# Graph attention in three layers: units of up to five chunks, weights in SBUF, second PSUM banks for R

## The chip, the cores and the metric

The kernel runs on one core of a Trainium2 chip. The time is device microseconds of one execution, from several executions of the same program. Five engines work side by side and meet at semaphores: TensorE (PE; its weight loads are listed as PEld), VectorE (DVE), ScalarE (ACT), GpSimd (POOL) and SyncE (SP). SP and POOL issue the DMAs: SP the plain ones, POOL the gathers of rows by an index list.

## The reference, cut to what matters

Four layers run over a graph of 3327 nodes with 512 features: `x = x + layer(relu(layernorm(x)), adj)`. Layers 0, 2 and 3 are graph attention with 8 heads of 64, layer 1 averages neighbours. The attention of layer 3, to which the others are alike:

```python
hp = jnp.einsum('nd,hdf->hnf', h, W)
f_src = jnp.einsum('hnf,hf->hn', hp, a_src)
f_dst = jnp.einsum('hnf,hf->hn', hp, a_dst)
e = jax.nn.leaky_relu(f_src[:, :, None] + f_dst[:, None, :], ALPHA)
e = jnp.where(adj[None] > 0, e, NEG_FILL)
att = jax.nn.softmax(e, axis=-1)
out = jnp.einsum('hij,hjf->hif', att, hp)
```

The adjacency is sparse and skewed: a node's chance of an edge falls with its number, so the first nodes have many neighbours and the last ones few.

## The kernel before

Since the exponential of a leaky ReLU of a sum is the larger of two products, each factor known per node, the weight of an edge from j to i is, but for factors of i that the softmax divides out, the larger of a value R of the target i and a value T of the source j, times exponentials that are put into the source's row beforehand. So each layer first writes a `table` with one row of 528 numbers per node: 8 heads x (64 features + 1), scaled, and 8 values T. (Layer 0 has 104 further words per row with the adjacency as bits.) R goes to `r_dram` in one form and stays in SBUF as `r3`, three bf16 parts, in another.

Targets are taken in groups of 64 (`GB`), two groups to a block of 128, 52 groups in all. `PLAN` gives for each group how many chunks of 128 source rows it reads: `dense` (128 consecutive nodes, a plain DMA), `mixed` and `pure` (gathers by the index list). There are 368 chunks per layer: 150 dense and mixed ones, called slots, where a source may reach any of the 64 targets, and 218 pure ones, where each row is one edge. `Lists.units` (L585) cuts a group's slots into units of at most `SLOTS` and its edges into units of at most `UNIT`, as even as can be. `ls.order` alternates blocks with many chunks and blocks with few.

`attend` (L1347) runs over the units in that order, for layers 0, 2 and 3. The order of the instructions on TensorE, VectorE and ScalarE is the order in which the code records them; GpSimd and SP run ahead on their own queues until a buffer is not free.

- `load` (L1444) fetches a unit's rows into `rows_e` (edges) or `rows_s` (slots), three units ahead in the text; how far the gathers run ahead in time is a matter of the buffers.
- A slot unit: VectorE takes the larger of R, broadcast to all partitions in PSUM as `r_bc` by `spread` (L1374), and T, into `mx` in PSUM (L1581), and multiplies by the 0/1 mask into `wgt` in SBUF (L1585). TensorE multiplies, head by head, `wgt` by the rows and adds into `facc` (L1616; 16 instructions a chunk).
- An edge unit: `pick` (L1506) selects R of each edge's target with a 0/1 matrix `edges` on TensorE, into `r_of` in PSUM, two units ahead; `summed` (L1517) adds R's three parts into `w_of` on VectorE, just behind the work of the unit before; then the larger of `w_of` and T (L1568), and `vw`, the rows times that weight (L1571). TensorE sums `vw` over the targets with the 0/1 matrix `ones_of` (L1605; 4 instructions a chunk).
- In layer 0 the 0/1 matrices are made from the bits: `bits` (L1461, VectorE), `masks` (L1478 to L1483, ScalarE), and for edges `turned` (L1493, TensorE) and `kept` (L1502, ScalarE and a DMA), three units ahead. Layers 2 and 3 read what layer 0 kept.
- At a group's end `ending` copies the sums (L1419), divides (L1425, L1432) and goes through the layer's finish (L1656 to L1663), one step per unit, called by `later`.
- `tick`, called once per unit too, drives work for the next layer: in layer 0 batch statistics with 26 GpSimd operations `bn_d` (L1715), in layer 2 the projection of finished blocks (`Following`), eight steps a block; the next block starts when the one before has taken `lag` steps. When the loop is over, `hurry` gives it three PSUM banks of the loop's and the remaining blocks follow.

PSUM has eight banks. In layer 2 they are two of `facc`, two of `mx`, one `r_bc`, one `r_of`, two of the projection. `w_of` shares `mx`'s buffer (`mx[:, 0, :UNIT, :H]`).

## Time and profile before

| | us |
|---|---|
| median of 4 runs | 2625.29 (2622.69 to 2633.84) |
| the profiled execution | 2648.22 |
| its span | 2646.4 |
| lists and the projection of layer 0 | 0 to about 337 |
| loop of layer 0 | 337 to 896 |
| batch statistics, layer 1 | 896 to 1512 |
| loop of layer 2 | 1512 to 2079 |
| the last projections of layer 2 | 2079 to 2125 |
| loop of layer 3 and its end | 2123 to 2646 |

The span runs from the first to the last instruction of the program; the execution's time has what lies around it as well. Engine busy times overlap. "Idle" in the profile is an engine's time without work just ahead of an instruction, and the arrow names what ended most of it; an end of a matmul is modelled there, so that a wait for TensorE is often put down to the instruction beside the one that released it. DMA_INDIRECT is one gather of 128 rows; its duration is GpSimd's part, not the transfer.

The DMA issues of the loops, by size:

```profile
rows_s<-table SPq DMA_DIRECT2D x46, 528.0 KB
rows_s<-table SPq DMA_DIRECT2D x62, 264.0 KB
rows_e<-table,idx POOLq DMA_INDIRECT x654
rows_s<-table,idx POOLq DMA_INDIRECT x219
```

### The profile page before, as it was taken

The numbers are of one execution on the slowest core, as the hardware profiler recorded it, in microseconds if no ns is written. First come the engines' busy times: TensorE is split into PE (matmuls) and PEld (weight loads), VectorE is DVE, ScalarE is ACT, GpSimd is POOL, SyncE is SP. The second block draws the span as 40 slices with busy tenths as digits, with TensorE's granted clock in tenths as the row PEclk, the third lists the DMA queues.
The fourth block names the chain that finished last, engine by engine and source line by source line (L and its number), as shares of the span: only waits on it lengthen the run. The fifth ranks groups of instructions, "written<-read, shape, count | busy, mean of one in ns | idle before, by whom it ended". The sixth has DMA issues, their size and how long they took to land. (4 is left out here: it accounts for less than half of the span.)

```text
span 2646.4 us, 42809 instructions
## 1 busy us (share of the span) xinstructions
PE 2006.4 (76%) x14843; PEld 1126.9 (43%) x14843; DVE 1698.6 (64%) x3056; ACT 1095.6 (41%) x4124; POOL 1152.0 (44%) x1205
## 2 busy tenths in 40 slices
PE   5887767778777499778989758888888756767675
PEld 4654344445444243223333245454444344444342
DVE  5567867776667680234454567777767467878776
ACT  3564113445454452122222204567777503344343
POOL 0000045566555202655666345554555045555552
PEclk9788868888888799989999877788888867777676
DMA  7685188767767384756777787776767177777773
GB/s 310 232 303 165 62 296 245 236 205 220 210 202 236 102 276 160 234 180 203 224 226 235 226 243 212 223 211 203 212 210 217 50 256 225 246 229 214 213 244 96
DMA packets 204943, 561.86 MB, mean 212 GB/s; under 512 B 36985, under 2 KB 42745, under 8 KB 201392
## 3 DMA queue, kind: packets, MB, share of 16 engines
q0 software_dynamic: 93120, 327.86, 41.1%
q1 hardware_dynamic: 111600, 231.20, 25.8%
q8 instruction: 120, 1.97, 0.3%
q14 instruction: 103, 0.84, 0.1%
HBM read 496.07 MB, written 62.86 MB: 211 GB/s over the span
## 5 line engine op out<-in xcount | busy, mean ns | idle before, releaser
L1342 POOL DMA_INDIRECT rows_e<-table,idx x654 | 623.8, 954 | 716.0 <-DMA rows_s<-table 330.6
L1605 PE MATMUL facc<-vw,ones_of 128*64 128x260 f32 x2616 | 501.2, 488 | 100.7 <-DVE vw L1571 59.6
L1616 PE MATMUL facc<-rows_s,wgt 128*64 128x65 f32 x7200 | 403.9, 257 | 225.8 <-issue 137.8
L1616 PEld LDWEIGHTS facc<-rows_s,wgt 128*64 128x64 f32 x7200 | 335.6, 165 | 348.2 <-issue 228.5
L1342 POOL DMA_INDIRECT z_rows<-z_dram,idx x291 | 277.1, 952 | 299.4 <-DMA z_dram<-z_out 130.9
L1571 DVE TENSOR_TENSOR vw<-rows_e,w_of 128x1040 f32<-128x1040 f32 (+1 forms) x270 | 395.7, 1466 | 9.3
L1342 POOL DMA_INDIRECT rows_s<-table,idx x219 | 211.8, 967 | 395.7 <-PE facc L1616 235.5
L1585 DVE TENSOR_TENSOR wgt<-mx,mask 128x1024 f32<-128x1024 f32 (+1 forms) x255 | 280.3, 1099 | 86.9 <-ACT mask L1483 26.2
L1581 DVE TENSOR_TENSOR mx<-r_bc,rows_s 128x1024 f32<-128x1024 f32 (+1 forms) x255 | 280.6, 1100 | 74.3 <-DMA rows_s<-table 16.3
L1605 PEld LDWEIGHTS facc<-vw,ones_of 128*64 128x64 f32 x2616 | 215.3, 166 | 255.4 <-issue 159.4
L1432 ACT ACTIVATE fhp<-sums,rd 64x64 f32<-64x64 f32 x816 | 215.6, 334 | 228.8 <-DVE rd L1425 152.3
L1523 DVE TENSOR_REDUCE w_of<-r_of 128x16 f32<-128x48 f32 (+1 forms) x270 | 61.4, 227 | 230.1 <-PE r_of L1515 57.3
L1866 PE MATMUL sage_acc<-z_rows,z_mask 128*64 128x512 f32 x622 | 167.2, 607 | 9.5 <-DMA z_rows<-z_dram,idx 7.1
L1849 ACT CAST z_mask<-mask 128x128 f32<-128x128 uint8 (+1 forms) x201 | 51.2, 287 | 231.0 <-PE sage_acc L1866 135.4
L921 PE MATMUL p_wh<-fWt,hT 128*128 128x512 f32 x208 | 107.5, 665 | 39.0 <-ACT hT L916 32.0
L1419 ACT COPY sums<-facc 128x260 f32<-128x260 f32 x153 | 56.3, 368 | 192.3 <-PE facc L1616 145.6
L739 PE MATMUL wh_ps<-fWt,hT 128*128 128x512 f32 x208 | 116.3, 711 | 0.0
L1515 PE MATMUL r_of<-r_three,edges 64*128 64x24 bf16 x654 | 61.0, 178 | 64.2 <-ACT edges L1502 31.8
L1432 ACT ACTIVATE bn_y<-sums,rd 64x64 f32<-64x64 f32 x408 | 107.7, 334 | 2.6 <-DVE rd L1425 1.0
L978 PE MATMUL p_wh<-fWt,hT 128*128 128x512 f32 x184 | 106.7, 733 | 0.6 <-issue 0.6
L1502 ACT CAST edges<-st_ps 64x384 bf16<-64x384 f32 (+1 forms) x90 | 37.0, 411 | 162.1 <-PE st_ps L1493 75.2
L1817 DVE TENSOR_TENSOR s_o<-n_ps,sage_b 128x512 f32<-128x512 f32 x26 | 18.0, 690 | 132.8 <-PE n_ps L1814 76.1
(252 smaller groups left out, 2949.2 us busy)
## 6 DMA issues: line engine op xcount, KB each, us to landing
adj_i<-in_adj SPq DMA_DIRECT2D x26, 1664.0 KB
rows_s<-table SPq DMA_DIRECT2D x46, 528.0 KB
table<-v_row SPq DMA_DIRECT2D x78, 264.0 KB
rows_s<-table SPq DMA_DIRECT2D x62, 264.0 KB
rows_s<-table SPq DMA_DIRECT2D x23, 632.0 KB
fin_x<-fx SPq DMA_DIRECT2D x52, 256.0 KB
rows_e<-table,idx POOLq DMA_INDIRECT x654
rows_s<-table SPq DMA_DIRECT2D x31, 316.0 KB
```

The source lines that it names most:

```text
L739: nc.tensor.matmul(wh, hT[:, kc, :], self.Wt[:, kc, :], start=(kc == 0), stop=(kc == KC - 1))
L921: nc.tensor.matmul(wh, hT[:, kc, :], self.Wt[:, kc, :], start=(kc == 0), stop=(kc == KC - 1))
L978: nc.tensor.matmul(wh, hT[:, kc, :], self.Wt[:, kc, :], start=(kc == 0), stop=(kc == KC - 1))
L1342: nc.gpsimd.indirect_dma_start(out=dst, out_offset=None, in_=src[:, :], in_offset=bass.IndirectOffsetOnAxis(ap=idx[:, k : k + 1], axis=0))
L1432: nc.scalar.mul(hp[o0 : o0 + GB, h * F : (h + 1) * F], sm[mine, q, 0:F], rd[mine, q, :])
L1523: nc.vector.tensor_reduce(w[:, :n], re[:, :n].rearrange("p k (t h) -> p k h t", h=H), AX.X, ALU.add)
L1571: nc.vector.tensor_tensor(vw[:, :n], gt[:, :n, : H * (F + 1)].rearrange("p k (h x) -> p k h x", x=F + 1), w[:, :n].unsqueeze(3).to_broadca ...
L1581: nc.vector.tensor_tensor(mx[:, :n], rbs[j].unsqueeze(1).to_broadcast(full), T.unsqueeze(3).to_broadcast(full), ALU.max)
L1585: nc.vector.tensor_tensor(wt[:, :n], mx[:, :n], mk.unsqueeze(2).to_broadcast(full), ALU.mult)
L1605: nc.tensor.matmul(accs[g][v * GB : (v + 1) * GB, :sw].rearrange("p (q x) -> p q x", x=F + 1), ones_of[i][:, k, :], by[:, v], start=f, stop=l,
L1616: nc.tensor.matmul(accs[g][v * GB : (v + 1) * GB, q * (F + 1) : (q + 1) * (F + 1)], wt[:, k, h, :], gt[:, k, h * (F + 1) : (h + 1) * (F + 1)],
L1866: nc.tensor.matmul(acc[u * GB : (u + 1) * GB, :], m, z, start=f, stop=l)
```

## The change

`SLOTS` and `UNIT` are now given by layer: slot units of up to 2, 3 and 4 chunks and edge units of up to 4, 5 and 5 in layers 0, 2 and 3, where they were 2 and 3 in all. `mx` is gone: the larger of R and T is written into `wgt` in SBUF and multiplied by the mask in place. `w_of` is an SBUF tile of its own. The two banks of `mx` go to a second `r_bc` and a second `r_of`. Row buffers: edges 3 (were 5 in layer 0 and 6 in the others), slots 4 (4 and 5); `vw` and `wgt` have 2 everywhere (were 3 in layers 2 and 3); `ones_of` 4 (5). `lag` in layer 2 is 4 (5), and `hurry` hands over one bank of `r_of` and two of `r_bc`.

```diff
--- before.py
+++ after.py
@@ -68,8 +68,7 @@
 NSHIFT = 8
 LNB = 5
 ROW = H * (F + 1) + H
-UNIT = 3
-SLOTS = 2
+SLOTS, UNIT = {0: 2, 2: 3, 3: 4}, {0: 4, 2: 5, 3: 5}
 AHEAD = 3
 HOT = 2
 EPARTS = 5
@@ -582,11 +581,11 @@
         src += [(False, k * HALF + g) for k in range(pure)]
         return [(self.at[g] + i, d, k) for i, (d, k) in enumerate(src)]
 
-    def units(self, g):
+    def units(self, g, slots, unit):
 
         dense, mixed, pure = PLAN[g]
         rows, out = self.rows(g), []
-        for edge, part, most in ((False, rows[: dense + mixed], SLOTS), (True, rows[dense + mixed :], UNIT)):
+        for edge, part, most in ((False, rows[: dense + mixed], slots), (True, rows[dense + mixed :], unit)):
             n, at = -(-len(part) // most), 0
             for b in range(n):
                 w = len(part) // n + (b < len(part) % n)
@@ -1350,11 +1349,11 @@
 
 
 
-        width = table.shape[1]
+        width, slots, unit = table.shape[1], SLOTS[layer], UNIT[layer]
         groups = [b * PG + u for b in ls.order for u in range(PG)]
         units = []
         for j, g in enumerate(groups):
-            mine = ls.units(g)
+            mine = ls.units(g, slots, unit)
             spread_at = sum(not e for e, _, _ in mine) - 1
             units += [(j, g, e, rows, s0, i == 0, i == len(mine) - 1, i == spread_at) for i, (e, rows, s0) in enumerate(mine)]
         hq = H // PG
@@ -1363,7 +1362,7 @@
             name=f"facc_ps{layer}", bufs=2, space=PSUM
         ) as aps, tc.manual_schedule(engines={ET.PE, ET.DVE, ET.Activation}):
             loaded, ones_of, st_of, found, w_of, rrs, rbs, accs, ends, over = {}, {}, {}, {}, {}, {}, {}, {}, [], []
-            ahead = 2
+            ahead, wide = 2, 2
 
             def fetch(j):
                 if j < len(groups):
@@ -1375,7 +1374,7 @@
 
 
                 if j < len(groups):
-                    rb = aps.tile([P, H * GB], F32, name="r_bc", tag="r_bc", bufs=1)
+                    rb = aps.tile([P, H * GB], F32, name="r_bc", tag="r_bc", bufs=wide)
                     nc.tensor.matmul(rb, ones[0:2, :].bitcast(F32R), rrs.pop(j).bitcast(F32R), start=True, stop=True)
                     rbs[j] = rb.rearrange("p (h i) -> p h i", i=GB)
 
@@ -1446,9 +1445,9 @@
                 if i < len(units):
                     _, _, e, rows, _, _, _, _ = units[i]
                     if e:
-                        gi = ap.tile([P, UNIT, width], I32, name="rows_e", tag="rows_e", bufs=5 if layer == 0 else 6)
+                        gi = ap.tile([P, unit, width], I32, name="rows_e", tag="rows_e", bufs=3)
                     else:
-                        gi = ap.tile([P, SLOTS, width], I32, name="rows_s", tag="rows_s", bufs=4 if layer == 0 else 5)
+                        gi = ap.tile([P, slots, width], I32, name="rows_s", tag="rows_s", bufs=4)
                     loaded[i] = gi
                     take(gi, table, rows)
 
@@ -1457,7 +1456,7 @@
                 if layer == 0 and i < len(units):
                     _, g, _, rows, _, _, _, _ = units[i]
                     n, nw = len(rows), GB // WB
-                    on = ap.tile([P, UNIT, nw, WB], U16, name="on", tag="on")
+                    on = ap.tile([P, unit, nw, WB], U16, name="on", tag="on")
                     nc.vector.tensor_tensor(
                         on[:, :n],
                         loaded[i][:, :n, ROW:].bitcast(U16)[:, :, g * nw : (g + 1) * nw].unsqueeze(3).to_broadcast([P, n, nw, WB]),
@@ -1473,7 +1472,7 @@
                     n, m0 = len(rows), rows[0][0]
                     mk = mask[:, m0 : m0 + n, :]
                     if e:
-                        so = ones_of[i] = ap.tile([P, UNIT, GB], F32, name="ones_of", tag="ones_of", bufs=5)
+                        so = ones_of[i] = ap.tile([P, unit, GB], F32, name="ones_of", tag="ones_of", bufs=4)
                         if layer == 0:
                             nc.scalar.activation(so[:, :n, :], on, AF.Sign)
                             nc.scalar.copy(mk, so[:, :n, :])
@@ -1488,7 +1487,7 @@
                     _, g, _, rows, _, _, _, _ = units[i]
                     u = g % PG
                     mine = slice(u * GB, (u + 1) * GB)
-                    st = st_of[i] = aps.tile([P, UNIT, P], F32, name="st_ps", tag="st_ps", bufs=1)
+                    st = st_of[i] = aps.tile([P, unit, P], F32, name="st_ps", tag="st_ps", bufs=1)
                     for k in range(len(rows)):
                         nc.tensor.matmul(st[mine, k, :], ones_of[i][:, k, :], cs["ident"], start=True, stop=True)
 
@@ -1498,7 +1497,7 @@
                     _, g, _, rows, s0, _, _, _ = units[i]
                     u, n = g % PG, len(rows)
                     mine = slice(u * GB, (u + 1) * GB)
-                    to = ap.tile([P, UNIT, P], BF16, name="edges", tag="edges", bufs=3)
+                    to = ap.tile([P, unit, P], BF16, name="edges", tag="edges", bufs=3)
                     nc.scalar.copy(to[mine, :n, :], st_of[i][mine, :n, :])
                     nc.sync.dma_start(edges_dram[mine, s0 : s0 + n, :], to[mine, :n, :])
                     st_of[i] = to[mine, :n, :]
@@ -1510,7 +1509,8 @@
                     b, u = divmod(g, PG)
                     mine = slice(u * GB, (u + 1) * GB)
                     st = st_of.pop(i) if layer == 0 else edges[mine, s0 : s0 + len(rows), :]
-                    re = found[i] = aps.tile([P, UNIT, 3 * H], F32, name="r_of", tag="r_of", bufs=1)
+                    bank = aps.tile([P, BANK], F32, name="r_of", tag="r_of", bufs=wide)
+                    re = found[i] = bank[:, : unit * 3 * H].rearrange("p (k x) -> p k x", x=3 * H)
                     for k in range(len(rows)):
                         nc.tensor.matmul(re[:, k, :], st[:, k, :], r3[mine, b, :], start=True, stop=True)
 
@@ -1518,8 +1518,7 @@
 
                 if i < len(units) and units[i][2]:
                     n, re = len(units[i][3]), found.pop(i)
-                    mx = aps.tile([P, SLOTS, H, GB], F32, name="w_of", tag="mx", bufs=1)
-                    w = w_of[i] = mx[:, 0, :UNIT, :H]
+                    w = w_of[i] = ap.tile([P, unit, H], F32, name="w_of", tag="w_of")
                     nc.vector.tensor_reduce(w[:, :n], re[:, :n].rearrange("p k (t h) -> p k h t", h=H), AX.X, ALU.add)
 
             for j in range(2):
@@ -1566,7 +1565,7 @@
                 if e:
                     w = w_of.pop(i)
                     nc.vector.tensor_tensor(w[:, :n], w[:, :n], T, ALU.max)
-                    vw = ap.tile([P, UNIT, H, F + 1], F32, name="vw", tag="vw", bufs=2 if layer == 0 else 3)
+                    vw = ap.tile([P, unit, H, F + 1], F32, name="vw", tag="vw")
                     full = [P, n, H, F + 1]
                     nc.vector.tensor_tensor(
                         vw[:, :n],
@@ -1577,12 +1576,11 @@
                 else:
                     mk = mask[:, m0 : m0 + n, :]
                     full = [P, n, H, GB]
-                    mx = aps.tile([P, SLOTS, H, GB], F32, name="mx", tag="mx", bufs=1)
+                    wt = ap.tile([P, slots, H, GB], F32, name="wgt", tag="wgt")
                     nc.vector.tensor_tensor(
-                        mx[:, :n], rbs[j].unsqueeze(1).to_broadcast(full), T.unsqueeze(3).to_broadcast(full), ALU.max
+                        wt[:, :n], rbs[j].unsqueeze(1).to_broadcast(full), T.unsqueeze(3).to_broadcast(full), ALU.max
                     )
-                    wt = ap.tile([P, SLOTS, H, GB], F32, name="wgt", tag="wgt", bufs=2 if layer == 0 else 3)
-                    nc.vector.tensor_tensor(wt[:, :n], mx[:, :n], mk.unsqueeze(2).to_broadcast(full), ALU.mult)
+                    nc.vector.tensor_tensor(wt[:, :n], wt[:, :n], mk.unsqueeze(2).to_broadcast(full), ALU.mult)
                 summed(i + 1)
                 early(i)
                 if begins:
@@ -1630,9 +1628,7 @@
                     ends.append(ending(g))
             over.append(True)
             if beside is not None:
-                mx = aps.tile([P, SLOTS, BANK], F32, name="mx", tag="mx", bufs=1)
-                rb = aps.tile([P, BANK], F32, name="r_bc", tag="r_bc", bufs=1)
-                beside.hurry((mx[:, 0, :], mx[:, 1, :], rb))
+                beside.hurry([aps.tile([P, BANK], F32, name=k, tag=k, bufs=wide) for k in ("r_of", "r_bc", "r_bc")])
             while ends or (beside is not None and beside.busy()):
                 later()
 
@@ -1875,7 +1871,7 @@
     edges = epool.tile([P, ls.ne, P], BF16, name="edges")
     with ExitStack() as l3:
         at2 = proj
-        proj = following(l3, 3, 2, t["L3_gnn_W"], 2, 5)
+        proj = following(l3, 3, 2, t["L3_gnn_W"], 2, 4)
         attend(2, at2.table, at2.r_dram, at2.r3, elu_into(x2, x3, proj.begin), proj.tick, beside=proj, edges=edges)
     attend(3, proj.table, proj.r_dram, proj.r3, elu_into(x3, out), edges=edges)
```

## The prediction

> **What bounds the kernel now.** I read the page's totals first, then the busy time of each engine by stretch, then the groups of instructions with shapes kept apart, then the waits, then the timeline instruction by instruction.
>
> ```profile
> span 2646.4 us, 42809 instructions
> PE 2006.4 (76%) x14843; PEld 1126.9 (43%) x14843; DVE 1698.6 (64%) x3056; ACT 1095.6 (41%) x4124; POOL 1152.0 (44%) x1205
> ```
> ```profile
> core 0: us, PE busy (x) PEld busy (x) DVE busy (x) ACT busy (x) POOL busy (x), PEclk, DMA share, GB/s
> 336.60:896.00 559.40, 408.54 (x4065) 266.80 (x4067) 393.76 (x664) 248.44 (x832) 307.96 (x316) 0.83 0.72 220
> 1511.70:2078.90 567.20, 452.81 (x4022) 270.54 (x4023) 405.07 (x699) 331.84 (x1339) 276.69 (x288) 0.81 0.70 212
> 2078.90:2125.50 46.60, 24.54 (x71) 12.40 (x67) 14.58 (x44) 17.07 (x84) 5.02 (x6) 0.72 0.21 79
> 2122.90:2627.00 504.10, 346.13 (x3541) 216.19 (x3541) 388.55 (x539) 174.14 (x589) 276.19 (x288) 0.73 0.73 223
> ```
>
> The three attention loops (layers 0, 2, 3) take 559 + 567 + 504 = 1630 us, 62% of the span; the change touches nothing else, except the 46.6 us between the last matmul of layer 2's loop and the first of layer 3's. No engine is full in them. VectorE (DVE) works 70%, 71% and 77% of the three loops, TensorE 73%, 80% and 69%; the rest is waiting of one for the other.
>
> ```profile
> L1523 DVE TENSOR_REDUCE w_of<-r_of 128x16 f32<-128x48 f32 x156 | 33.8, 217 | 165.8 <-remote 45.2 <-PE r_of L1515 45.0 <-PE facc L1616 24.0
> L1523 DVE TENSOR_REDUCE w_of<-r_of 128x24 f32<-128x72 f32 x114 | 27.6, 242 | 64.4 <-PE facc L1616 28.5 <-PE r_of L1515 12.3 <-PE st_ps L1493 9.8
> L1568 DVE TENSOR_TENSOR w_of<-w_of,rows_e 128x16 f32<-128x16 f32 x156 | 28.3, 182 | 3.1 <-DVE rd L1425 0.4 <-DVE w_of L1523 0.3
> L1571 DVE TENSOR_TENSOR vw<-rows_e,w_of 128x1560 f32<-128x1560 f32 x114 | 202.8, 1779 | 3.9
> L1571 DVE TENSOR_TENSOR vw<-rows_e,w_of 128x1040 f32<-128x1040 f32 x156 | 192.9, 1237 | 5.4
> L1585 DVE TENSOR_TENSOR wgt<-mx,mask 128x1024 f32<-128x1024 f32 x195 | 238.8, 1225 | 64.9 <-PE facc L1616 20.6 <-remote 18.8 <-ACT mask L1483 11.5
> L1585 DVE TENSOR_TENSOR wgt<-mx,mask 128x512 f32<-128x512 f32 x60 | 41.5, 692 | 21.9 <-ACT mask L1483 14.7 <-PE facc L1616 2.5 <-issue 2.1
> L1662 DVE SCALAR_TENSOR_TENSOR fin_x<-fhp,fin_x 128x512 f32<-128x512 f32 x52 | 35.7, 687 | 6.6 <-ACT fin_x L1658 6.6
> ```
>
> The figure after the first bar is busy time, then ns of one; after the second bar, idle time just before. Two rows of one operation give its fixed part: vw costs 1779 - 1237 = 542 ns a chunk, so 1237 - 2 x 542 = 153 ns whatever its size; wgt 533 ns a chunk and 159 ns fixed (mx alike: 1226 and 692); the reduce 25 ns a chunk and 167 fixed; the maximum on w_of 189 - 182 = 7 ns a chunk and 168 fixed. VectorE's idle time stands almost wholly before the reduce, 165.8 + 64.4 = 230 us, and there TensorE is late with r_of.
>
> **Fewer instructions.** Counted from the plan, a layer's 175 units become 154, 128 and 120. Edge units fall from 90 to 69, 59 and 59, slot units from 85 to 85, 69 and 61. An edge unit less saves 153 + 167 + 168 = 488 ns of VectorE, a slot unit less 2 x 159 = 318 ns; in layer 0 an edge unit also has its bit test (345 ns for two chunks, 366 for three), some 0.30 us each. Layer 0: 21 x 0.79 = 16.6 us. Layer 2: 31 x 0.488 + 16 x 0.318 = 20.2. Layer 3: 31 x 0.488 + 24 x 0.318 = 22.8. Matmuls, gathers and bytes stay as many. A saved VectorE microsecond counts only where VectorE sets the pace; I take its busy shares above: 11.7 + 14.4 + 17.5 = **-44 us** (ends: 0 if TensorE paces all of it, -60 if VectorE does). ScalarE's fewer copies are cost at nothing: it is busy 44%, 59% and 35%; without that cover they would be a gain.
>
> **Fewer waits.** 270 edge units become 187, so the 230 us before the reduce would shrink by 83/270, 71 us, if each wait were a price per unit. TensorE's work behind them is unchanged, so I take a quarter: **-18** (ends 0 and -71). The second r_of bank by itself gives little: TensorE waited for the reduce 13 us in layers 2 and 3. The second r_bc bank: nothing, no row shows a wait for it.
>
> **The new operands.** mx and w_of lay in PSUM; now the product with the mask, the maximum on w_of and vw read two SBUF operands each. For VectorE that is no change: L1662 reads two SBUF tiles and takes 687 ns, wgt with one in PSUM 692. On 215 + 2 x 187 = 589 instructions 5 ns are -3 us, taken as 0. [...]
>
> **What it does to GpSimd's gathers.** The timeline of layer 3:
>
> ```profile
> 2396.05 0.68 DVE L1662 SCALAR_TENSOR_TENSOR fin_x<-fhp,fin_x 128x512 f32<-128x512 f32 x1
> 2396.37 1.18 POOL L1342 DMA_INDIRECT rows_s<-table,idx  x1 [1.47 <-PE r_of L1515]
> 2396.77 0.69 DVE L1663 SCALAR_TENSOR_TENSOR fin_x<-fin_e,fin_x 128x512 f32<-128x512 f32 x1
> 2397.59 1.78 DVE L1571 TENSOR_TENSOR vw<-rows_e,w_of 128x1560 f32<-128x1560 f32 x1
> 2397.86 0.95 POOL L1342 DMA_INDIRECT rows_s<-table,idx  x1 [0.31 <-issue]
> ```
>
> A gather takes 0.95 us. This one began inside L1662, which reads two SBUF tiles, and took 1.18: it ended 0.81 us after L1662's end at 2396.73. L1663, which began later, did not lengthen it and was not lengthened. The gather at 2397.86 began inside vw, one operand then in PSUM, and took 0.95. So a gather that starts inside a VectorE instruction with two SBUF operands waits for its end, less some 0.13 us. After the change such instructions fill, in layer 3, vw 28 x 1.78 + 21 x 2.32 + 10 x 2.86 = 127 us, products 90, maxima 12, L1662 and L1663 36: 265 of 504 us, 0.525. By squares of these lengths the mean rest at a random instant is 0.87 us; 0.525 x (0.87 - 0.13) = 0.39 us a gather, 111 us on 288 gathers. GpSimd now needs 288 x (0.95 + 0.30 between two) = 360 us; it would need 471 of 504. By the same arithmetic layer 0 gets 79 us more (477 of 559, with its bn_d work) and layer 2 95 (459 of 567). All 285 us lie beside other work as long as GpSimd runs ahead; what runs out first is layer 3. Ends: 0, and 285. I take 12 us in layer 3, 3 in layer 2, 4 in layer 0: **+19**. And in layer 0 GpSimd's 26 tensor operations bn_d of 1.3 us can hold VectorE: the bit test L1461, two SBUF operands, has a median of 286 ns and a longest of 1181. At most 26 x 0.65 = 17 us; I take **+6**.
>
> [...]
>
> **Starts, ends, buffers.** The first unit of layer 3 has four chunks in place of two, of layer 2 three: 2 and 1 more chunks of 264 KB at 223 and 212 GB/s, 2.4 + 1.2 us, and 2 x 533 ns a chunk more before the first matmul, 2.1 + 1.1: **+7**. In the tail of layer 2, TensorE's order has four blocks' projections left after the last facc matmul where it had three, because the background steps once per unit and the later blocks have only four units. 46.6 us / 3.5 blocks is 13 us more there; its work leaves the loop, where TensorE is 80% busy, for which I give back 7: **+6** (ends 0, +13). The lag of 4 instead of 5 keeps the rate of one block in four steps. Three edge buffers of 4 or 5 chunks hold as many groups in the middle as six of 2 did; SP's fewer, larger loads (its queue, L1337 and L1371, waits for TensorE as before) I cost at nothing.
>
> **Sum:** -44 - 18 + 19 + 6 + 7 + 6 = **-24 us**, against the profiled 2648.2 us (span 2646.4) 2624. That execution lies 23 us over the median of 2625.29; the terms are fixed times, so the forecast for the median is 2601.
>
> **Rivals.** (1) GpSimd becomes the bound: gathers wait behind vw and the products, and rows come late, first in layer 3's light groups, where four to five gathers fall to some 7 to 8 us. [...] At a quarter: -43 + 71 = +28, **2653**. For it: 471 of 504 us leaves no room for jitter. Against: GpSimd now waits 235 us for rows_s buffers, so it does run ahead. (2) Larger units take the hand-overs with them: in two-unit groups the edge matmuls of one group lie under the slot work of the next, and a third of the 230 us goes, -77 in place of -18: -83, **2542**. For it: the waits stand before the reduce. Against: light groups that already have two units still show VectorE 70 to 74% busy. (3) TensorE paces the loops, so only a third of the 44 comes through, -15, with no fewer waits, +8 of gathers and +13 at the ends: +6, **2631**, no change.
>
> **Chances.** Forecast 0.36, (2) 0.20, (3) 0.12, (1) 0.32. 0.3%, 8 us, is about what a measurement of this kernel can tell from no change. So faster 0.56, same 0.12, slower 0.32. The range runs to 2535 below and 2660 above; the forecast's own is 2580 to 2617.
>
> **What will show it.** Mean gather time in the loops: 0.95 us if operands in SBUF do not matter, 1.2 to 1.35 by the arithmetic above. VectorE's busy time should fall by some 60 us in all; the idle time before the reduce should fall below 212; the tail of layer 2 should grow to about 59 us. If the gathers' mean rises and VectorE's idle time moves before the maximum or the slots' first operation with a gather as releaser, rival 1 decides. I am wrong if TensorE's clock moves by several hundredths: I took it as unchanged.

## The result, and the profile after

The changed kernel takes 2640.53 us (median of 42 runs, 2615.72 to 2660.25), the kernel before beside it 2629.2 us (63 runs); the ratio is 1.0041, with a 95% interval of 1.0024 to 1.0058. It is slower by some 11 us where 24 us less was forecast; the time lies in the range, the sign is wrong. (Ratios leave out runs that lie over 1.5% above the fastest of their kernel; in the fourth experiment that left three of six and in the ninth eight of twelve, so their medians are given too.)

The profiled execution took 2611.25 us, less than any of the 42, and that of before 2648.22, one of the slower. So busy times and waits are compared below, and loops of these two only with care. The page's totals:

```profile
span 2609.4 us, 41596 instructions
PE 1958.5 (75%) x14843; PEld 1096.4 (42%) x14843; DVE 1643.9 (63%) x2707; ACT 1080.9 (41%) x3991; POOL 1421.0 (54%) x1205
```

VectorE has 55 us less to do than before, GpSimd 269 us more for as many instructions. The table by stretches, layer 0's loop and then layers 2 and 3 with the tail between them, each from its first facc matmul to its last:

```profile
core 0: us, PE busy (x) PEld busy (x) DVE busy (x) ACT busy (x) POOL busy (x), PEclk, DMA share, GB/s
335.10:898.70 563.60, 400.34 (x4073) 258.93 (x4075) 387.42 (x579) 241.72 (x770) 380.08 (x314) 0.82 0.72 218
1503.80:2590.40 1086.60, 788.94 (x7629) 481.90 (x7629) 751.90 (x1013) 516.38 (x1944) 744.75 (x576) 0.78 0.71 215
```

Over the same stretches, before has 557.9 and 1113.0. Layer 0 got longer even in this short execution. If each execution's distance from its median is spread evenly over it, an estimate is 16 us more for layer 0 and 6 less for layers 2 and 3. The groups (after the second bar, idle time just before and what ended most of it), first two rows of before, then the kernel after:

```profile
L1342 POOL DMA_INDIRECT rows_e<-table,idx x654 | 623.8, 954 | 716.0 <-DMA rows_s<-table 330.6 <-issue 170.8 <-DMA r_two<-r_dram 98.5
L1461 DVE TENSOR_TENSOR on<-rows_e,fbit 128x192 uint16<-128x192 uint16 (+1 forms) x90 | 31.8, 354 | 0.4 <-ACT ones_of L1478 0.2
```
```profile
L1341 POOL DMA_INDIRECT rows_e<-table,idx x654 | 825.3, 1262 | 650.8 <-DVE on L1460 332.3 <-issue 185.3 <-DMA r_two<-r_dram 103.6
L1522 DVE TENSOR_REDUCE w_of<-r_of 128x24 f32<-128x72 f32 (+3 forms) x187 | 44.8, 240 | 95.9 <-PE facc L1614 30.6 <-remote 17.5 <-PE r_bc L1378 16.2
L1567 DVE TENSOR_TENSOR w_of<-w_of,rows_e 128x24 f32<-128x24 f32 (+3 forms) x187 | 40.7, 218 | 97.1 <-DMA rows_e<-table,idx 83.0 <-issue 12.6
L1460 DVE TENSOR_TENSOR on<-rows_e,fbit 128x192 uint16<-128x192 uint16 (+2 forms) x69 | 29.9, 434 | 100.2 <-DMA rows_e<-table,idx 95.0 <-issue 5.2
```

A gather of rows_e takes 1.26 us where it took 0.95 (of rows_s 1.24). VectorE's idle time before the reduce fell from 230 to 96 us, but 97 us stand now before the maximum on w_of (4.8 before) and 100 before the bits of single edges (0.4 before); both wait for gathered rows. Of the 97 us, 93 lie in layer 3; the bits exist in layer 0 alone. What that looks like in layer 0, on VectorE and on GpSimd (start, duration, in brackets the idle time before):

```profile
466.87 1.78 DVE L1570 TENSOR_TENSOR vw<-rows_e,w_of 128x1560 f32<-128x1560 f32 x1
...
469.05 1.78 DVE L1570 TENSOR_TENSOR vw<-rows_e,w_of 128x1560 f32<-128x1560 f32 x1
...
472.54 1.23 DVE L1583 TENSOR_TENSOR wgt<-wgt,mask 128x1024 f32<-128x1024 f32 x1
473.68 0.28 DVE L1460 TENSOR_TENSOR on<-rows_s,fbit 128x128 uint16<-128x128 uint16 x1
479.43 0.36 DVE L1460 TENSOR_TENSOR on<-rows_e,fbit 128x192 uint16<-128x192 uint16 x1 [5.46 <-DMA rows_e<-table,idx]
```
```profile
468.00 1.48 POOL L1341 DMA_INDIRECT rows_s<-table,idx  x1 [0.62 <-PE r_bc L1378]
469.78 1.87 POOL L1341 DMA_INDIRECT rows_e<-table,idx  x1 [0.30 <-issue]
471.96 0.94 POOL L1341 DMA_INDIRECT rows_e<-table,idx  x1 [0.30 <-issue]
473.21 1.38 POOL L1341 DMA_INDIRECT rows_e<-table,idx  x1 [0.30 <-issue]
```

The vw that ends at 468.65 frees the buffer that the unit three edge units later needs. That unit's three gathers start at 469.78, after one for rows_s, and end at 474.59; VectorE wants its bits at 473.96 and gets them at 479.43. The first gather began inside a vw and ended 0.82 us after it, the third inside a mask product, also 0.82 us after its end; each was lengthened, none for the whole of the other. So it is in all three loops: the 409 gathers that began inside a VectorE instruction with two SBUF operands ended 0.82 us (median) after it, and 203 during which such an instruction began took 0.95 us, at most 0.97.

From all units of layer 0 in the traces: from the end of a unit's last gather to the start of its bits passed 14.8 us (median) before and 4.0 after. The shortest after is 2.7. At 31 of the 69 units VectorE stood idle before the bits, at none of 90 before. The slack is gone.

### The profile page after: what moved, and what is told of

Its sections match the earlier page's. It is cut to its first block, busy times and chain, and to the rows that moved or that the text cites. A ratio compares the mean times of both kernels' runs of the same rounds, so it can differ in the third digit from the quotient of the medians.

```text
span 2609.4 us, 41596 instructions
## 1 busy us (share of the span) xinstructions
PE 1958.5 (75%) x14843; PEld 1096.4 (42%) x14843; DVE 1643.9 (63%) x2707; ACT 1080.9 (41%) x3991; POOL 1421.0 (54%) x1205
## 5 line engine op out<-in xcount | busy, mean ns | idle before, releaser
L1341 POOL DMA_INDIRECT rows_e<-table,idx x654 | 825.3, 1262 | 650.8 <-DVE on L1460 332.3
L1570 DVE TENSOR_TENSOR vw<-rows_e,w_of 128x1560 f32<-128x1560 f32 (+3 forms) x187 | 385.0, 2059 | 6.5
L1341 POOL DMA_INDIRECT rows_s<-table,idx x219 | 271.4, 1239 | 203.4 <-PE facc L1614 115.2
L1580 DVE TENSOR_TENSOR wgt<-r_bc,rows_s 128x1024 f32<-128x1024 f32 (+3 forms) x215 | 272.1, 1266 | 89.9 <-PE facc L1614 23.1
L1583 DVE TENSOR_TENSOR wgt<-wgt,mask 128x1024 f32<-128x1024 f32 (+3 forms) x215 | 277.7, 1292 | 31.6 <-ACT mask L1482 15.9
L1492 PE MATMUL st_ps<-fident,ones_of 128*64 128x128 f32 x436 | 75.2, 318 | 73.1 <-issue 43.5
L920 PE MATMUL p_wh<-fWt,hT 128*128 128x512 f32 x208 | 102.0, 636 | 18.0 <-issue 13.6
L1522 DVE TENSOR_REDUCE w_of<-r_of 128x24 f32<-128x72 f32 (+3 forms) x187 | 44.8, 240 | 95.9 <-PE facc L1614 30.6
L1378 PE MATMUL r_bc<-r_two,fones 2*128 2x512 f32 x156 | 89.3, 572 | 13.4 <-DMA edges<-edges_dram 4.7
L1862 PEld LDWEIGHTS sage_acc<-z_rows,z_mask 128*64 128x64 f32 x622 | 47.7, 137 | 119.4 <-issue 97.4
```

The lines of the kernel that those rows point to most:

```text
L920: nc.tensor.matmul(wh, hT[:, kc, :], self.Wt[:, kc, :], start=(kc == 0), stop=(kc == KC - 1))
L1341: nc.gpsimd.indirect_dma_start(out=dst, out_offset=None, in_=src[:, :], in_offset=bass.IndirectOffsetOnAxis(ap=idx[:, k : k + 1], axis=0))
L1378: nc.tensor.matmul(rb, ones[0:2, :].bitcast(F32R), rrs.pop(j).bitcast(F32R), start=True, stop=True)
L1492: nc.tensor.matmul(st[mine, k, :], ones_of[i][:, k, :], cs["ident"], start=True, stop=True)
L1570: nc.vector.tensor_tensor(vw[:, :n], gt[:, :n, : H * (F + 1)].rearrange("p k (h x) -> p k h x", x=F + 1), w[:, :n].unsqueeze(3).to_broadca ...
L1580: nc.vector.tensor_tensor(wt[:, :n], rbs[j].unsqueeze(1).to_broadcast(full), T.unsqueeze(3).to_broadcast(full), ALU.max)
```

## The experiments

Eighteen runs went to five chips, and the kernel before ran beside them on each: 2599.4 us on the chip of runs 1 to 4, 2325.0 (5 to 8), 2621.3 (9 to 12), 2614.4 (13 to 15) and 2328.2 (16 to 18). So ratios are compared, and "first kind" and "quick" name the two sorts of chip. Expectations in us without a ratio were written for a before of some 2630; on the first chip 1% must be taken off. Ratios, where nothing else is said, were expected for a chip of the first kind.

**1 to 4: where the operands lie, or how the units are cut.** Run 1 is the changed kernel with w_of beside r_of:

```diff
-                    re = found[i] = bank[:, : unit * 3 * H].rearrange("p (k x) -> p k x", x=3 * H)
+                    re = bank[:, : unit * 3 * H].rearrange("p (k x) -> p k x", x=3 * H)
+                    found[i] = re, bank[:, BANK // 2 : BANK // 2 + unit * H].rearrange("p (k h) -> p k h", h=H)
...
-                    n, re = len(units[i][3]), found.pop(i)
-                    w = w_of[i] = ap.tile([P, unit, H], F32, name="w_of", tag="w_of")
+                    n, (re, w) = len(units[i][3]), found.pop(i)
+                    w_of[i] = w
```

> The changed kernel, with the unit's weights w_of written into the free half of the PSUM bank that holds r_of; so the maximum and the multiplication into vw (41 + 385 us of VectorE) have one operand in SBUF again, and only the mask product (278 us) has two. Theory A (gathers that start inside a VectorE instruction with two SBUF operands wait for its end, and rows come late): the mean gather of rows_e falls from 1262 ns to about 1080, GpSimd's busy time by about 160 us, VectorE's idle time before the maximum from 97 us to under 50, and the time from 2640 to 2600 to 2618 us. Theory B (three edge buffers in place of five or six: rows are asked for too late, whatever a gather takes): the gathers shorten too, but the wait for rows before the maximum stays above 75 us and the time at 2633 to 2645. Theory C (a unit of five chunks is too coarse: everything behind it waits for its last chunk): as B.

0.9951 (0.9916 to 0.9985), against 1.0041 unedited (on another chip). Gathers take 1060 ns, GpSimd 1244.7 us, the wait before the maximum is gone, that before the bits is 51 us, layer 0's loop 536 us. That is theory A, with the time, 2590.74 us, at the upper end of its range. Run 2 puts the same operands into the kernel before:

```diff
-                    mx = aps.tile([P, SLOTS, H, GB], F32, name="w_of", tag="mx", bufs=1)
-                    w = w_of[i] = mx[:, 0, :UNIT, :H]
+                    w = w_of[i] = ap.tile([P, UNIT, H], F32, name="w_of", tag="w_of", bufs=2)
...
-                    mx = aps.tile([P, SLOTS, H, GB], F32, name="mx", tag="mx", bufs=1)
+                    wt = ap.tile([P, SLOTS, H, GB], F32, name="wgt", tag="wgt", bufs=2 if layer == 0 else 3)
...
```

> The kernel before, with nothing of the change but the place of the weights: w_of in an SBUF tile of its own, the slots' maximum written into the SBUF tile wgt and multiplied there. Units, edge buffers and single PSUM banks stay. Theory A: the mean gather of rows_e rises from 954 to 1200 to 1270 ns, GpSimd's busy time by 250 us or more, and the time from 2631 to 2650 to 2690 us. Theory B (edge buffers) and theory C (unit size): gathers may be slower, but with five and six buffers of three chunks they stay covered, and the time is 2625 to 2638.

0.9828 (0.9793 to 0.9863): quicker by 1.7%, though gathers rose to 1167 ns and GpSimd by 197 us. Neither theory had that. With five and six buffers slow gathers cost nothing here. Run 3 goes the other way, large units with w_of and mx in PSUM (layer 2 has no banks for mx):

```diff
-            ahead, wide = 2, 2
+            ahead, wide = 2, 2 if layer == 2 else 1
...
+                    mx = wt if layer == 2 else aps.tile([P, slots, H, GB], F32, name="mx", tag="mx", bufs=1)
...
```

> The changed kernel's units and edge buffers, with all weights made in PSUM again in layers 0 and 3 (as before, in one tile mx of two or four banks, with single banks for r_bc and r_of), and in layer 2 w_of in PSUM and the mask product in SBUF. Theory A: the mean gather of rows_e falls to 960 to 1040 ns, GpSimd's busy time to about 1180 to 1230 us, and the time to 2585 to 2612 us. Theories B and C: the time stays at 2630 to 2650, with the waits for rows before the maximum and before the bits (97 and 95 us) still above 75 us each.

0.9992 (0.9959 to 1.0025), gathers 995 ns, wait before the bits 42 us: the gathers and waits of theory A, but a time, 2594.58 us, between its range and that of B and C. So large units and fewer buffers, almost alone, are worth nothing here. Run 4 undoes them in layer 0 only:

```diff
-SLOTS, UNIT = {0: 2, 2: 3, 3: 4}, {0: 4, 2: 5, 3: 5}
+SLOTS, UNIT = {0: 2, 2: 3, 3: 4}, {0: 3, 2: 5, 3: 5}
...
-                        gi = ap.tile([P, unit, width], I32, name="rows_e", tag="rows_e", bufs=3)
+                        gi = ap.tile([P, unit, width], I32, name="rows_e", tag="rows_e", bufs=5 if layer == 0 else 3)
```

> The changed kernel, with layer 0's units of single edges at three chunks and five edge buffers as before; layers 2 and 3 and the weights in SBUF as changed. Theories B and C, as far as they act in layer 0: its idle time of VectorE before the bits for lack of rows falls from 95 us to under 60, its loop by 10 to 20 us, and the time from 2640 to 2618 to 2630. Theory A: gathers in layer 0 stay as slow (about 1.25 us a chunk), the saved buffering is small beside it, 16 or so more units cost VectorE some 10 us, and the time is 2633 to 2650.

Medians 2586.17 and 2599.4, 0.995 (the ratio is 0.9816, 0.9765 to 0.9866). Layer 0's loop falls from 563.6 to 530 us and the wait before the bits from 95 to 11.5, while gathers stay at 1284 ns. So in layer 0 it is units or buffers.

**5 to 8: buffers, banks, and a chip on which all is different.** Run 5 is run 2 with `bufs=3` for rows_e and 4 for rows_s and ones_of; run 6 is run 2 with `bufs=2` for r_of and r_bc; run 7 the changed kernel; run 8 run 2 without the edit to w_of.

> The kernel of the second experiment (units of before, weights in SBUF, ratio 0.983 to before), with the changed kernel's numbers of buffers: three for rows_e in place of five and six, four for rows_s in place of five in layers 2 and 3, four for ones_of. Theory B now (too few buffers: gathers made slow by VectorE's two SBUF operands are harmless as long as enough units are on their way): the ratio rises from 0.983 to 1.000 to 1.015, layer 0's loop from 530 us to 550 or more. Theory C now (large units: a unit can start only when its last chunk is there, and a buffer comes free only when all of it was used): the ratio stays at 0.980 to 0.990 and layer 0's loop under 540 us.

> The kernel of the second experiment with second PSUM banks for r_of and r_bc, the change's third part, and nothing else. If the banks carry part of the gain: VectorE's idle time before the reduce falls from 194 us to under 130 and the ratio from 0.983 to 0.965 to 0.978. If not: the idle time falls but comes back elsewhere, and the ratio is 0.979 to 0.990.

> The changed kernel as it is, beside the others on their chip, with a second profile. Both theories: ratio 0.998 to 1.010, layer 0's loop 555 to 575 us, layers 2 and 3 with the tail 1080 to 1105 us. A ratio under 0.995 would say that the loss is a matter of the chip on which it was measured.

> The kernel before, with only the slots' half of the second experiment: the maximum is written into the SBUF tile wgt and multiplied there, w_of stays in PSUM in the tile mx. If the gain of the second experiment comes from the slots' weights (the mask product reads SBUF and one tile less is passed on): ratio 0.980 to 0.988, and the mean gather about 1050 ns. If it comes from w_of's own tile, which no longer shares mx: ratio 0.995 to 1.002.

1.0865 (1.084 to 1.0891), 1.0292 (1.0268 to 1.0315), 1.0719 (1.0686 to 1.0752) and 0.9983 (0.9969 to 0.9996): on a quick chip the change costs 7%. Of these only run 8 is where an expectation had it. The stretch of layer 0 in runs 5 and 6:

```profile
336.70:959.50 622.80, 447.22 (x4074) 284.53 (x4075) 402.01 (x663) 253.25 (x840) 359.76 (x314) 0.74 0.63 197
```
```profile
335.60:839.80 504.20, 377.15 (x4074) 245.33 (x4075) 393.55 (x663) 249.97 (x835) 383.99 (x314) 0.86 0.77 244
```

The columns are those of the stretches above. With three buffers layer 0 takes 119 us longer; units are those of before, so theory C falls there. The runs differ in the banks and in one buffer of ones_of too; the banks turn out small (runs 13, 14). TensorE's granted clock falls from 0.86 to 0.74, and the same 4074 matmuls keep it busy 70 us longer. So late rows come with a slower TensorE; what the wait and the clock cost each was not separated. The changed kernel's loops, 566 and 1027 us, stand against 461 and 949 in run 8. Here w_of's place costs as well: layer 0 takes 504 us in run 6, 461 in run 8 with single banks, and 462 in run 16, which has second banks, w_of in PSUM and layer 0's units and row buffers of before.

**9 to 12: how many buffers.** Theory D names the mechanism. The bits of single edges are made three units ahead, so where edge units follow one another, with three buffers a unit's gathers can start only in the step that wants its bits. Runs 9 and 10 are run 4 with 4 and with 3 in place of 5; run 11 is run 4 with run 1's edit; run 12 is run 6 with run 1's edit.

> The changed kernel with layer 0's units of single edges at three chunks and four buffers for rows_e there: the same bytes of SBUF as three buffers of four chunks. Theory D (in layer 0 VectorE makes the bits of unit i+3 in step i, while a third buffer comes free only when vw of unit i was made in that same step, so the gathers of i+3 start just when their rows are wanted): with a fourth buffer the gathers start one unit earlier, VectorE's idle time before the bits for rows_e falls from 95 us to under 40, and layer 0's loop is 25 us or more shorter than in the run with three buffers of three chunks beside it; ratio at least 0.01 lower than that run's. Theory B' (buffers count only by their bytes, as chunks on their way): the same as the changed kernel, both ways within 0.005.

> The changed kernel with layer 0's units of single edges at three chunks and its three buffers for rows_e. Theory D: three buffers are one too few whatever the unit's size; smaller units then cost more, since fewer chunks are on their way: layer 0's loop 580 to 640 us, VectorE's idle time before the bits for rows_e above 95 us, ratio 1.010 to 1.035 on a chip like the first, 1.075 or more where the kernel before takes 2325 us. Theory C (large units are the cost): layer 0's loop under 550 us and the ratio below the changed kernel's.

> The changed kernel with both suspected costs taken out: w_of in the free half of r_of's PSUM bank, as in the first experiment, and in layer 0 units of three chunks with five buffers, as in the fourth. If slow gathers and late buffers are the whole of the loss: ratio 0.975 to 0.990 on a chip like the first, and at most 1.02 where the kernel before takes 2325 us, layer 0's loop within 15 us of the best seen on that chip. If the large units of layers 2 and 3 cost in themselves: their loops and the tail stay 30 us or more above those of the run with small units beside it, and the ratio is above that run's by 0.01 or more.

> The kernel before with the two parts of the change that look free: second PSUM banks for r_of and r_bc, the slots' weights made in place in the SBUF tile wgt; w_of stays in PSUM, in the free half of r_of's bank; units and edge buffers as before. If the gathers set the time: mean gather 1.0 to 1.08 us, ratio 0.975 to 0.990 on a chip like the first and 0.985 to 0.998 where the kernel before takes 2325 us, where w_of in SBUF with the same banks had 1.029. If the second banks cost something in themselves: above 1.005.

Run 9: 0.9941 (0.9899 to 0.9983; by the medians, 2610.84 and 2621.34, 0.996), layer 0 540 us. Run 10: 1.0257 (1.0216 to 1.0297), 626 us. VectorE's wait by rows, in 9 and in 10:

```profile
DVE on L1460 <- DMA rows_e<-table,idx: 34.7, 19, 6.2
```
```profile
DVE on L1460 <- DMA rows_e<-table,idx: 170.4, 40, 6.7
```

(us, times, longest.) One buffer more, the only difference of the two, takes 0.032, some 83 us (74 by the medians), off the time; four buffers of three chunks have the bytes of the change's three of four. Theory D holds: every sign that it named came. From the last gather to the bits are 4.2 us with three buffers, 5.8 with four, 9.6 with five.

Run 11: 0.9951 (0.9919 to 0.9982), as run 1 and run 9. The two remedies do not add up on this kind of chip: they cure the same lateness. Neither sign that was set for run 11 came (0.975 to 0.990, or 0.01 above run 12). Run 12: 0.9887 (0.985 to 0.9923). It has run 11's layer 0 in units and edge buffers, but units and buffers of before in layers 2 and 3, and is the quicker, so there the large units gained nothing. VectorE's groups before the slots' maximum and the reduce, run 11 and then run 12:

```profile
L1581 DVE TENSOR_TENSOR wgt<-r_bc,rows_s 128x1024 f32<-128x1024 f32 (+3 forms) x215 | 272.0, 1265 | 206.1 <-PE facc L1615 64.1 <-PE facc L1604 49.6 <-remote 21.1
L1523 DVE TENSOR_REDUCE r_of<-r_of 128x24 f32<-128x72 f32 (+3 forms) x208 | 49.9, 240 | 148.2 <-PE facc L1615 40.2 <-remote 38.5 <-PE r_of L1516 33.2
```
```profile
L1582 DVE TENSOR_TENSOR wgt<-r_bc,rows_s 128x1024 f32<-128x1024 f32 (+1 forms) x255 | 277.1, 1087 | 101.7 <-PE facc L1616 42.3 <-remote 28.2 <-DMA rows_s<-table 13.3
L1524 DVE TENSOR_REDUCE r_of<-r_of 128x16 f32<-128x48 f32 (+1 forms) x270 | 60.2, 223 | 224.1 <-PE facc L1616 55.2 <-remote 47.2 <-PE r_of L1517 47.1
```

Waiting for TensorE moved from the reduce (224 to 148 us) to the slots' maximum (102 to 206).

**13 to 15: runs 2, 6 and 8 on one chip.**

> The kernel of the second experiment once more (units, buffers and single banks of before, w_of and the slots' weights in SBUF), to stand on one chip beside the next two. If w_of's place costs where the kernel before takes 2325 us (there w_of in SBUF with second banks had 1.029 and w_of in PSUM with single banks 0.998): 1.015 to 1.035 on such a chip. On a chip like the first: 0.979 to 0.988 again.

> The same with second PSUM banks for r_of and r_bc. If the banks are worth nothing either way: within 0.004 of the run before this one. If they cost (the second bank lets r_of be picked earlier, which no one needs): 0.01 or more above it. If they gain: 0.005 or more below it, with VectorE's idle time before the reduce under 130 us.

> The kernel of the eighth experiment once more: only the slots' weights in SBUF, w_of in PSUM, single banks. On a chip like the first: 0.983 to 0.990 if the slots' half carries the gain of the second experiment, 0.995 to 1.002 if w_of's own tile does. On a chip where the kernel before takes 2325 us: 0.998 again.

0.986 (0.9816 to 0.9903), 0.9826 (0.9783 to 0.9868) and 0.9905 (0.9873 to 0.9937). The slots' weights in SBUF gain 1% here, w_of's place adds 0.5%, the banks 0.3%; the last two are not clear of their intervals. Run 14's kernel had 1.0292 as run 6: it is the chip that turns the sign.

**16 to 18: the best of both, and the slots' units.** Run 16 is run 11 again; run 17 adds `bufs=3` for wgt in layer 3; run 18 has `SLOTS` 2 in layers 2 and 3 with three wgt buffers.

> The kernel of the eleventh experiment (w_of in PSUM, layer 0 at three chunks and five buffers, large units in layers 2 and 3) once more, as the base for the next two on their chip: 0.990 to 1.000 on a chip like the first, layers 2 and 3 with the tail about 1100 us, VectorE's idle time before the slots' maximum about 200 us.

> The same with a third buffer for wgt in layer 3 (four chunks each; in layer 2 there is no room for it). Theory E (the change took wgt from three buffers to two in layers 2 and 3; as the maximum is now written into wgt, it must wait until TensorE is through with a whole unit of up to four chunks): VectorE's idle time before the maximum falls by 40 us or more, layer 3's loop by 10 to 25 us, and the ratio by 0.004 to 0.010 against the base. Theory F (the wait is TensorE's pace and only shows there): the idle time moves to the mask product or the reduce, and the ratio stays within 0.003 of the base.

> The base with the slots' units of layers 2 and 3 at two chunks and three buffers for wgt there, as before the change; units of single edges stay at five chunks. Theory E: as small slot units free wgt earlier, the idle time before the maximum falls from about 200 us to 130 or less, and the ratio to 0.984 to 0.991, that of the run with all units small; some 40 more slot units cost VectorE 13 us of busy time. Theory F: the busy time comes on top, ratio 0.996 to 1.004.

These fell on a quick chip: 0.9882 (0.9858 to 0.9906), 0.9884 (0.9862 to 0.9906) and 0.9927 (0.9906 to 0.9948). Run 16's kernel beats that of before on either kind of chip (run 11), and the changed one, which ran on other chips of both kinds. There is little wait left for a third wgt buffer to cure, so run 17 doesn't decide theory E where the wait was 206 us. In run 18, 40 more slot units cost VectorE 13.5 us of busy time, and the median is 10 us longer: the busy time comes on top, as theory F has it, but here too there was little wait that theory E could have cured. Run 16's groups beside run 11's, the same kernel:

```profile
L1581 DVE TENSOR_TENSOR wgt<-r_bc,rows_s 128x1024 f32<-128x1024 f32 (+3 forms) x215 | 271.6, 1263 | 45.2 <-DMA rows_s<-table 18.6 <-PE r_bc L1378 16.2 <-DMA r_two<-r_dram 7.9
L1523 DVE TENSOR_REDUCE r_of<-r_of 128x24 f32<-128x72 f32 (+3 forms) x208 | 49.4, 238 | 14.1 <-PE r_of L1516 13.8
L1615 PE MATMUL facc<-rows_s,wgt 128*64 128x65 f32 x7200 | 340.1, 248 | 173.4 <-DVE wgt L1584 110.6 <-issue 33.0 <-ACT sums L1418 14.6
```

And run 11's row of TensorE:

```profile
L1615 PE MATMUL facc<-rows_s,wgt 128*64 128x65 f32 x7200 | 397.6, 256 | 248.5 <-issue 149.0 <-DVE wgt L1584 73.6 <-ACT sums L1418 11.4
```

On the quick chip VectorE hardly waits for TensorE. On the other TensorE sits 149 us before these matmuls with nothing awaited ("issue"), in 182 stops, half of them of 0.5 us or less and the longest of 5.0, and VectorE waits with it.

What a quick chip's loops run into instead is GpSimd. In layer 3 the kernels of run 16 and run 7, on two quick chips, differ in w_of's place alone; its loop in run 16 and in run 7:

```profile
1863.20:2279.40 416.20, 295.25 (x3541) 190.10 (x3541) 352.62 (x396) 171.86 (x558) 309.77 (x284) 0.80 0.83 265
```
```profile
2003.70:2483.10 479.40, 307.62 (x3541) 194.87 (x3541) 353.22 (x397) 172.27 (x560) 373.81 (x284) 0.76 0.74 230
```

With up to 0.30 us between two gathers, 85 us in all, GpSimd's 310 and 374 us (the column with x284) become 395 of 416 and 459 of 479: 64 us more of gathers, 63 us more of loop. Counted so, runs 8 and 6 have 393 of 410 and 426 of 444 there. In layer 2, w_of's place takes GpSimd from 389 to 463 us and the loop from 458 to 493. So on a quick chip slower gathers come straight through. On the first kind the loops are longer, and except in layer 3 of the changed kernels GpSimd has more room in them (run 2: 469 of 531, 412 of 536 and 422 of 483 in layers 0, 2 and 3).

## Why the prediction was wrong

**The step that failed** is "Three edge buffers of 4 or 5 chunks hold as many groups in the middle as six of 2 did", cost at nothing, with 4 us for layer 0 among the +19. It counted chunks. What matters in layer 0 is how many units a gather may run ahead of the bits, which are made three units ahead. Four buffers of three chunks, the same bytes, bring the change from 1.0041 to 0.9941 (on another chip of its kind), 26 us, or 21 by the medians; w_of out of SBUF brings nearly the same, 24 us by run 1, across chips too. Without this loss the kernel is 10 to 16 us quicker than before, against 24 forecast, 12 of them for layer 0's larger edge units, which run 9 gives up; four buffers with units of four chunks were not run. The prediction looked for the lateness in layer 3 first, where "471 of 504" was tight. GpSimd was as full there as it said, 461 of 488 us counted with the steps between gathers, and VectorE waited 93 us; but the loop was no longer than before (488 against 502), and in run 1, where that wait is 5 us, layers 2 and 3 take 1078.5 us, 0.7% less on a chip 1.1% quicker. So on the first kind of chip the place was layer 0; on the quick chip it was all three loops.

**The -44 and the -18.** VectorE's busy time fell by 55 us, as counted (some 60), and the reduce's wait by far more than 18. That VectorE's idle time stood "almost wholly before the reduce" was a misreading: 230 of some 440 us in the three loops did. But on the first kind of chip none of it came through in layers 2 and 3: large units stand at 0.9951, small ones at 0.9887. This looks like rival 3, TensorE paces, and not by its work alone but by stops that the trace gives no reason for. On the quick chip the slot units' part does come through: those layers take 930 us in run 16, 947 with small slot units in run 18. What units and buffers did together can be read from run 14, which has the change's operands and banks with units and buffers of before: 0.9826 against 1.0041, across chips, and side by side on the quick chip (runs 6 and 7) 1.0292 against 1.0719. So the larger units and fewer buffers were a loss of 2% and of 4%. The two buffers of vw and wgt in place of three, and `lag`, were not tested alone there.

**The new operands, taken as 0.** VectorE's instructions last about as long as L1662's row had it (mask product 1125 ns in run 2, 1099 before). Yet with units and buffers of before the operands in SBUF gained 1.4 to 1.7% on the first kind of chip and, with second banks, lost 2.9% on the quick one. The gain of 10 to 16 us just given holds this gain. What brings it was not separated; shorter instructions do not: the five groups of edge and slot work (reduce, maximum on w_of, vw, slots' maximum, mask product) take 1076 us in run 2 and 1068 before.

**The gathers** were sized rightly: 1.24 to 1.26 us within the 1.2 to 1.35 expected, GpSimd +269 for +285. The gathers timed above were held at their start only, to 0.82 us after the other's end, as the row of before had shown (0.81 us), and not lengthened by one that began after them (0.95 us in 203 of them). What they cost on this kind of chip was asked of the wrong place.

**Rival 1** had the direction, slower, and half the mechanism: gathers behind vw and products, rows late, VectorE idle before the maximum. Its quarter is of the 285 us by which gathers were to lengthen, and its -43 is the -24 without the +19 for gathers; so 43 of the 285 us on the path, 15%, would make no change, and +11 takes about 54, 19%. But the share isn't a property of the gathers: with five and six buffers run 2, with gathers nearly as slow (1167 ns), lost nothing on the first kind of chip. On the quick chip rival 1 is right as it stands: in layer 3 the loop follows GpSimd. **Rival 2** saw the waits before the reduce vanish, and not that they would come back in other places. The **tail** of layer 2 grew from 46.2 to 54.8 us (59 expected), the clock stayed (0.831, 0.835).

## What to carry to other kernels

Count buffers in units of the loop, against how many units ahead the earliest consumer asks, before counting bytes: as many buffers as units of lead means that every load starts when it is wanted. When a change makes a transfer's issue slower and takes away buffers in the same edit, cost the two together, since each can be harmless alone. And a saving on one engine is worth what the pace of the others allows, which can differ between two chips by more than the change: work that hides where TensorE is slow can be paid in full where TensorE is quick and the next engine is the bound.

## What the runs showed of the hardware

- The kernel before takes 2599 to 2629 us on some chips and 2325 to 2328 on others, and one kernel's ratio goes from 0.983 to 1.029 between them. TensorE's unexplained idle time before slots matmuls, 149 us against 33 for the same kernel, goes with it, and so does the granted clock (0.836 and 0.885 in those runs). What makes the chips differ was not found; that the ratio turns goes with GpSimd's gathers, as above.
- Where TensorE stood idle longer, its granted clock was lower: 0.74 against 0.86 in layer 0 (runs 5 and 6; idle for 176 and 127 us), with 447 and 377 us for the same matmuls, and 0.76 against 0.84 (idle for 183 and 143 us), with 443 and 397 us, in runs 10 and 9, which differ in one buffer. How the idle time and the clock hang together, and what part of the 70 us comes from it, was not shown.
- The mean of a gather of rows_e follows the VectorE work with two SBUF operands: 954 ns with none of these products, 995 with layer 2's mask product, 1035 to 1072 with all mask products, 1112 to 1284 with w_of and vw too.
